# A graph-attention layer on one core: exponentials in mid-step, values 12 steps behind, and the last stage between the last steps

## The chip, the cores and the metric

The kernel runs on one core of a Trainium2 chip. A core has five engines that run their own instruction streams in order: PE (TensorE, matrix products; its weight loads are shown as PEld), DVE (VectorE), ACT (ScalarE), POOL (GpSimd) and SP (SyncE, here used only to issue DMAs). ACT and POOL issue DMAs too, each in its own stream. The metric is the device time of one execution in microseconds (us).

## The reference

One layer of a graph network: 12,500 nodes with 128 channels, 400,000 edges sorted by target node `dst`, 8 heads of 16 channels for the scores and 16 for the values.

```python
h = jnp.maximum(_layernorm(x, axis=-1), 0.0)
msg_src = h @ w_src + b_src
msg_dst = h @ w_dst
message = msg_src[edge_src] + msg_dst[edge_dst]
rad_w = _radial_mlp(edge_scalars, fc_w1, fc_b1, fc_w2, fc_b2, fc_w3, fc_b3)
message = message * edge_attr * rad_w
message = message @ w_sep + b_sep
msg_h = message.reshape(n_edges, H, AH + VH)
alpha = _smooth_leaky_relu(msg_h[:, :, :AH])
value = msg_h[:, :, AH:]
score = jnp.einsum('ehk,ahk->eh', alpha, alpha_dot)
att = _segment_softmax(score, edge_dst, n_nodes)[..., None]   # per target node
out = jax.ops.segment_sum(value * att, edge_dst, num_segments=n_nodes)
x = x + (out.reshape(n_nodes, H * VH) @ w_proj + b_proj)
```

## The kernel before

A first stage normalises the nodes and writes two tables to memory, `t_src` and `t_dst` (the two products of a node). It also counts into `bad` (`fits`, L310) whether the edges are sorted as the fast path needs; every engine then loads `bad` and branches into `windows` (L752).

`windows` walks the edges in steps. A section is 512 edges, a step takes a pair of sections (f = 0 and 1), and there are NP = 391 steps. `step(k)` (L1221) writes out by hand, in one order, what every engine does; several steps are in flight at once:

- two steps ahead POOL issues `gather(k + 2, f)` (L861), eight indirect DMAs a step of 128 rows of `t_src` each, into `gs0` and `gs1` with three buffers each;
- one or two steps ahead come the radial network (`mlp1`, `mlp2`, `mlp3`; silu on ACT), the one-hot rows of the targets and the split target rows (`split_md`);
- in the step itself PE turns the gathered rows into the PSUM tiles `pm0`, `pm1` (`sources`, L929) and adds the target rows (`message`, L937), and DVE multiplies into `mT` (L948), which is the message. `alphas` of the step before (PE, then a silu on ACT, L956) and `scores` every second step (PE, then an Identity on ACT, L987) give the scores;
- a block of MP = 8 steps shares one softmax. Its scores go through memory (`sc_d`) into one tile `S`. In the next block, with r = k mod 8: at the end of r = 2 `softmax_up` (a running maximum on DVE, L1008, over marks that PE spreads into the PSUM tile `m1`), at the end of r = 3 `softmax_down` (the same backwards, L1013) and `softmax_exp` (a subtraction on DVE, an Exp on ACT, L1020, and the maxima written to `max_d`), in r = 4 `softmax_T` in two halves (PE turns the exponentials, L1035, ACT copies them to `Pem`, L1038);
- LAG = 13 steps behind come `values` (PE, L1065, and a product with `Pem` on DVE, L1067) and, 14 behind, `sums` (PE, L1078) into a window of 64 rows for each section, which DVE copies to `ob` (L1082). SP stores the window to `win` and, twice 63 rows, to `agg` (`store`, L1088). The place in `agg` is a run-time value, so each store waits until the one before has landed.

`sums`, `softmax_T`, one half of `mlp1` and the block stages share one PSUM bank, `misc`.

Nodes whose edges lie across section ends are put right by 13 blocks of 128 window ends (`block_load` to `block_rows_out`, two Exps in `block_factors`). Eleven of them run inside the loop, 32 steps apart, and leave their rows in `obs_d`. `scatter(g)` (L1195), an indirect DMA on POOL, writes a block's rows to `agg`.

After the loop, 14 drain steps (k = 391 to 404) finish the values and sums. In each, `combined` brings a block's rows back and POOL scatters them. Then the last block is done, and `final` (L1392) runs over all nodes: it loads `agg` (128 values and 8 denominators a node) and `x` plus the bias (`xb`), divides (`quotients`, L1404), turns (PE and an ACT copy, L1427), multiplies with `w_proj` (PE, L1435), adds (DVE, L1438) and stores `out`.

Of the kernel before, what the change touches and what calls it, by code (L numbers as in the profile page):

```python
# [52 lines left out]
LAG = 13  # L53
# [3 lines left out]
def gnn_kernel(ctx: ExitStack, tc: tile.TileContext, a: dict, out: bass.AP):  # L57
# [9 lines left out]
    NX = -(-NP // MP) * MP * PR  # L67
    assert NT * P == E and RC * RP == E and NT % TPI == 0 and NT % SORT_T == 0
# [88 lines left out]
    with tc.tile_pool(name="node", bufs=2) as np_, tc.tile_pool(name="node1", bufs=1) as n1, \  # L157
# [25 lines left out]
        ends = n1.tile([NH, 17, 2], I32, name="ends")  # L183
        eb = n1.tile([P, NS, 2], I32, name="eb")
# [6 lines left out]
        def load_targets():  # L191
# [118 lines left out]
        def fits():  # L310
# [14 lines left out]
            nc.vector.tensor_copy(bad, sum_)  # L325
# [426 lines left out]
    def windows():  # L752
# [7 lines left out]
        with tc.tile_pool(name="ps", bufs=1, space=PSUM) as pp, \  # L760
# [255 lines left out]
            def softmax_exp(m):  # L1016
                M = Ms[m]
                nc.vector.tensor_sub(M[:, 0, :], S_all[m], M[:, 1, :])
                Ps[m] = sp.tile([P, SEC], F32, name="Pr", bufs=1)
                nc.scalar.activation(Ps[m], M[:, 0, :], AF.Exp)  # L1020
# [66 lines left out]

            def store(c, f):  # L1088
                at = nc.sync.value_load(base[0:1, f, c:c + 1])
                st = nc.sync.dma_start(out=agg[ds(at, W - 1), :], in_=accs[c][f * W:(f + 1) * W - 1, :])  # L1090
                if 2 * c + 1 >= (NC - 1) * (P // 2):
                    tc.declare_no_dep(st.ins, group="combined", reason="its rows follow those of the blocks")
# [45 lines left out]
            def block_maxima(g):  # L1138
                w, node = width(g), nodes.pop(g)
                differ[g] = sp.tile([P, P + 1], BF16, name="differ", bufs=1)  # L1140
# [11 lines left out]
            def block_factors(g):  # L1152
# [5 lines left out]
                nc.scalar.activation(de, de, AF.Exp)  # L1158
                nc.scalar.activation(mx, mx, AF.Exp)
                nc.vector.tensor_mul(mx[:, 1:w:2], mx[:, 1:w:2], differ.pop(g)[:, 1:w:2])  # L1160

            def block_columns(g):
# [7 lines left out]
                mx = mxs.pop(g)  # L1170
                tots[g] = [sp.tile([P, P], F32, name=n, bufs=2) for n in ("rn", "rd")]
# [23 lines left out]
            def scatter(g):  # L1195
# [6 lines left out]
                tc.add_to_no_dep_group("combined", st.ins)  # L1202

            comb = {}

            def combined(g):
                comb[g] = tail_pool.tile([P, ROW], F32, name="comb", bufs=2)
                return comb[g]

            stages = {0: lambda g: (block_load(g), block_rows(g)), 2: block_maxima, 4: block_factors,  # L1210
                      5: block_columns, 6: block_totals, 8: block_out}
            assert LAST_M * MP == (NC - 1) * SB and NP - LAST_M * MP < MP and LATE + (NC - 3) * SB + 8 < NP
# [8 lines left out]
            def step(k):  # L1221
# [63 lines left out]
                if has(c - 1):  # L1285
                    sums(c - 1)
                    if k >= NP:
                        store_win(c - 1)
# [39 lines left out]
                j, o = divmod(k - LATE, SB)  # L1328
                if 0 <= j < NC - 2 and o in stages:
                    stages[o](j)  # L1330

            for k in range(-5, NP):
                step(k)
            held.close()


            tail_pool = held.enter_context(tc.tile_pool(name="fin1", bufs=1, side="right"))
            x_fin = tail_pool.tile([P, NB, C], F32, name="x_fin")
            x_loads = load_xb(x_fin)
            last = NC - 1  # L1340

            def out_rows(g):
                block_rows_out(g, combined(g))
                scatter(g)

# [4 lines left out]
                5: lambda: block_load(last),  # L1350
                6: lambda: block_maxima(last),
                7: lambda: (block_factors(last), block_rows(last - 1)),
                8: lambda: block_columns(last - 1),
                9: lambda: block_totals(last - 1),
                10: lambda: out_rows(last - 1),
            }
            assert SB * (NC - 1) + LAG + 1 == NP + 7
            for k in range(NP, NP + LAG + 1):
# [9 lines left out]
            for _ in x_loads:  # L1368
                pass
            block_rows(last)  # L1370
            block_columns(last)
            block_totals(last)
            out_rows(last)
            work.close()
            with tc.tile_pool(name="fin", bufs=3) as fp:
                final(fp, x_fin, lambda i: pp.tile([P, 4, P], F32, name=("pm0", "pm1", "V")[i % 3]),
                      lambda i: pp.tile([P, 4, C], F32, name=("p3", "pa", "m1")[i % 3]))


    XQ = 12  # L1380
    out_v = out[0:NF * P, :].rearrange("(p t) c -> p t c", t=NF)
    agg_v = agg[0:NF * P, :].rearrange("(p t) c -> p t c", t=NF)

    def load_xb(x_fin):

        for t0, t1 in groups:
            nc.scalar.dma_start(out=x_fin[:, t0:t1, :], in_=xb_v[:, t0:t1, :])
            yield
        nc.scalar.dma_start(out=x_fin[:tail, NF, :], in_=xb[NF * P:N, :])
        yield  # L1390

    def final(fp, x_fin, turned, product):  # L1392
        starts = list(range(0, NB, XQ))
        gs, qs, qTs = {}, {}, {}

        def load_g(i):

            gs[i] = fp.tile([P, XQ, ROW], F32, name="g", bufs=len(starts))
            for n, t0, t1 in blocks(starts[i], min(starts[i] + XQ, NB)):
                o = starts[i]  # L1400
                nc.sync.dma_start(out=gs[i][:n, t0 - o:t1 - o, :],
                                  in_=agg_v[:, t0:t1, :] if n == P else agg[NF * P:N, :].unsqueeze(1))

        def quotients(i):  # L1404
            r = fp.tile([P, XQ, H], F32, name="r")
            qs[i] = fp.tile([P, XQ, C], F32, name="q")
            g = gs.pop(i)
            for n, t0, t1 in blocks(starts[i], min(starts[i] + XQ, NB)):
                s = slice(t0 - starts[i], t1 - starts[i])
                m = t1 - t0  # L1410
                nc.vector.tensor_scalar(r[:n, s, :], g[:n, s, C:ROW], 1e-16, None, op0=ALU.add)  # L1411
                nc.vector.reciprocal(r[:n, s, :], r[:n, s, :])  # L1412
                nc.vector.tensor_mul(  # L1413
                    qs[i][:n, s, :].rearrange("p t (h k) -> p (t h) k", h=H),
                    g[:n, s, 0:C].rearrange("p t (h k) -> p t h k", h=H),
                    r[:n, s, :].unsqueeze(3).to_broadcast([n, m, H, C // H]))

        def turn(i):
            t0, t1 = quads[i]
            q, o = qs[t0 // XQ], t0 // XQ * XQ  # L1420
            pt = turned(i)
            for t in range(t0, t1):
                n = rows(t)
                nc.tensor.transpose(pt[:, t - t0, :n], q[:n, t - o, :], ident[:n, :n])  # L1424
            w = (t1 - t0 - 1) * P + rows(t1 - 1)
            qTs[i] = fp.tile([P, 4, P], F32, name="qT")
            nc.scalar.copy(qTs[i].rearrange("p u n -> p (u n)")[:, :w], pt.rearrange("p u n -> p (u n)")[:, :w])  # L1427

        def finish(i):
            t0, t1 = quads[i]  # L1430
            qT = qTs.pop(i)
            py = product(i)
            for t in range(t0, t1):
                n = rows(t)
                nc.tensor.matmul(py[:n, t - t0, :], qT[:, t - t0, :n], w_proj, start=True, stop=True)  # L1435
            for n, u0, u1 in blocks(t0, t1):
                y = x_fin[:n, u0:u1, :]
                nc.vector.tensor_add(y, py[:n, u0 - t0:u1 - t0, :], y)  # L1438
                nc.sync.dma_start(out=out_v[:, u0:u1, :] if n == P else out[NF * P:N, :].unsqueeze(1), in_=y)

        for i in range(len(starts)):
            load_g(i)
        quotients(0)
        turn(0)
        for i in range(Q):
            if i % 3 == 1 and i // 3 + 1 < len(starts):
# [76 lines left out]
```

## Time and profile before

| | us |
|---|---|
| median of 3 runs | 4211.2 (4210.71 to 4215.71) |
| the profiled execution | 4210.06 |
| its span, first to last instruction | 4208.2 |
| busy in the span: PE, DVE, POOL, ACT | 3917.1, 3103.4, 3009.4, 1901.6 |

In the lines below, "L867" is a line of the kernel, "x8" a number of instructions, and a bracket holds how long the engine sat idle before the instruction and what ended the wait. A matrix product's end is modelled.

### The profile page before, as it was taken

The numbers are of one execution on the slowest core, as the hardware profiler recorded it, in microseconds if no ns is written. First come the engines' busy times: TensorE is split into PE (matmuls) and PEld (weight loads), VectorE is DVE, ScalarE is ACT, GpSimd is POOL, SyncE is SP. The second block draws the span as 40 slices with busy tenths as digits, with TensorE's granted clock in tenths as the row PEclk, the third lists the DMA queues.
The fourth block names the chain that finished last, engine by engine and source line by source line (L and its number), as shares of the span: only waits on it lengthen the run. The fifth ranks groups of instructions, "written<-read, shape, count | busy, mean of one in ns | idle before, by whom it ended". The sixth has DMA issues, their size and how long they took to land. (4 is left out here: it accounts for less than half of the span.)

```text
span 4208.2 us, 87881 instructions
## 1 busy us (share of the span) xinstructions
PE 3917.1 (93%) x29351; PEld 2391.0 (57%) x29351; DVE 3103.4 (74%) x6187; ACT 1901.6 (45%) x4549; POOL 3009.4 (72%) x3195
## 2 busy tenths in 40 slices
PE   6789999999999999999999999999999999999975
PEld 6345555555555555555555555555555555555555
DVE  5567777777777777777777777777777777777754
ACT  5344444444444444444444444444444444444421
POOL 4767777777777777777777777777777777777710
PEclk8999999999999999999999999999999999999988
DMA  7766777777776776777777776776777676776624
GB/s 249 233 173 187 191 187 187 197 192 180 199 192 179 196 195 174 195 195 188 188 192 194 181 193 180 178 188 182 178 191 184 183 184 183 188 180 180 184 84 160
DMA packets 593334, 783.08 MB, mean 186 GB/s; under 512 B 125554, under 2 KB 392303, under 8 KB 592741
## 3 DMA queue, kind: packets, MB, share of 16 engines
q1 hardware_dynamic: 384786, 514.16, 40.9%
q0 software_dynamic: 100416, 205.44, 23.6%
q10 hardware_dynamic: 107666, 57.76, 4.6%
q8 instruction: 234, 3.83, 0.4%
q14 instruction: 232, 1.89, 0.2%
HBM read 637.83 MB, written 139.30 MB: 185 GB/s over the span
## 5 line engine op out<-in xcount | busy, mean ns | idle before, releaser
L867 POOL DMA_INDIRECT gs<-t_src,idx x3125 | 2971.5, 951 | 978.8 <-issue 801.7
L956 ACT ACTIVATE sl<-pa,c_b_a 128x512 f32<-128x512 f32 x782 | 536.9, 687 | 1021.1 <-PE pa L954 1009.5
L961 DVE SCALAR_TENSOR_TENSOR al<-pa,sl 128x512 f32<-128x512 f32 x782 | 539.8, 690 | 596.6 <-ACT sl L956 577.1
L1065 PEld LDWEIGHTS V<-c_w_v,mT 128*128 128x128 f32 x6048 | 746.7, 194 | 292.1 <-DVE ob L1082 119.1
L1065 PE MATMUL V<-c_w_v,mT 128*128 128x128 f32 x6048 | 879.3, 289 | 0.0
L954 PE MATMUL pa<-mT,c_w_a 128*128 128x512 f32 x1564 | 816.1, 604 | 4.0 <-DVE mT L948 3.0
L1067 DVE TENSOR_TENSOR pvx<-V,Pem 128x512 f32<-128x512 f32 x756 | 517.7, 685 | 243.8 <-PE V L1065 232.0
L934 PEld LDWEIGHTS pm<-ident,gs 128*128 128x128 f32 x3125 | 393.0, 142 | 422.1 <-issue 316.9
L1078 PEld LDWEIGHTS misc<-pvx,oh 128*64 128x64 f32 x6250 | 353.0, 137 | 407.8 <-ACT h L890 392.7
L926 DVE SCALAR_TENSOR_TENSOR rad<-p,c_fc_b,w_b 128x512 f32<-128x512 f32 x782 | 550.0, 745 | 40.1 <-PE p L918 3.5
L1078 PE MATMUL misc<-pvx,oh 128*64 128x136 f32 x6250 | 454.2, 287 | 115.4 <-ACT h L890 108.2
L948 DVE SCALAR_TENSOR_TENSOR mT<-pm,c_b_src,rad 128x512 f32<-128x512 f32 x782 | 550.6, 746 | 2.2 <-PE pm L941 2.2
L904 ACT ACTIVATE h<-p,b 128x512 f32<-128x512 f32 x391 | 287.6, 735 | 422.7 <-PE p L901 367.9
L934 PE MATMUL pm<-ident,gs 128*128 128x128 f32 x3125 | 471.0, 273 | 0.0
L918 PE MATMUL p<-h,w3b 64*128 64x512 f32 x1564 | 405.2, 595 | 14.4 <-ACT h L904 14.4
L941 PE MATMUL pm<-ohT,m 64*128 64x512 bf16 x2346 | 321.8, 380 | 0.0
L987 ACT ACTIVATE Sp<-m,b_s 128x512 f32<-128x512 f32 x192 | 131.9, 687 | 393.9 <-PE m L970 389.8
L886 PE MATMUL m<-eT,w1b 64*128 64x256 f32 x782 | 274.3, 431 | 17.9 <-DVE M L1008 16.7
L886 PE MATMUL misc<-eT,w1b 64*128 64x256 f32 x782 | 274.3, 431 | 0.0
L1051 DVE TENSOR_TENSOR oh<-lane,misc 128x504 f32<-128x504 f32 x391 | 261.3, 668 | 0.0
L901 PE MATMUL p<-h,w2b 64*64 64x256 f32 x3128 | 259.7, 402 | 1.0 <-DVE rad L926 1.0
L954 PEld LDWEIGHTS pa<-mT,c_w_a 128*128 128x128 f32 x1564 | 242.2, 196 | 20.0 <-DVE mT L948 7.1
(172 smaller groups left out, 3651.0 us busy)
## 6 DMA issues: line engine op xcount, KB each, us to landing
w_b<-in_edge_weight SPq DMA_DIRECT2D x390, 512.0 KB
d_b<-in_dst SPq DMA_DIRECT2D x390, 256.0 KB
gs<-t_src,idx POOLq DMA_INDIRECT x3125
e_t<-in_edge_attr ACTq DMA_DIRECT2D x390, 128.0 KB
sc_d<-Sp SPq DMA_DIRECT2D x192, 256.0 KB
win<-ob SPq DMA_DIRECT2D x391, 68.0 KB
agg<-ob SPq DMA_DIRECT2D x782, 33.5 KB
md<-t_dst SPq DMA_DIRECT2D x782, 32.0 KB
```

Of the source, the lines that this page charges most:

```text
L867: nc.gpsimd.indirect_dma_start(out=gs[:, t, :], out_offset=None, in_=t_src[:, :], in_offset=bass.IndirectOffsetOnAxis(ap=idx[:, t0 + t:t0 ...
L886: nc.tensor.matmul(p1[q], w1b[s, :], eTs[k][s, :], start=True, stop=True)
L918: nc.tensor.matmul(p3s[k][:, f, 0:SEC], w3b[s, :], h2s[k][s, :], start=True, stop=True)
L926: nc.vector.scalar_tensor_tensor(rad[:, s], p3[:, f, 0:n], b3, w_g[k][:, s], op0=ALU.add, op1=ALU.mult)
L934: nc.tensor.matmul(pms[k, f][:, t * T:(t + 1) * T], gs[:, t, :], ident, start=(t == 0), stop=False, is_transpose=True, skip_group_check=True)
L948: nc.vector.scalar_tensor_tensor(mTs[k][:, s], pms.pop((k, f))[:, 0:n], b_n, rad[:, s], op0=ALU.add, op1=ALU.mult)
L954: nc.tensor.matmul(pa[:, 0:n], w_a, mTs[k][:, f * SEC:f * SEC + n], start=True, stop=True)
L956: nc.scalar.activation(sl[:, 0:n], pa[:, 0:n], AF.Silu, bias=b_a, scale=1.0)
L961: nc.vector.scalar_tensor_tensor(al, pa, 0.25, sl, op0=ALU.mult, op1=ALU.add)
L1065: nc.tensor.matmul(V[:, t, :], mTs[c][:, o:o + T], w_v, start=True, stop=True)
L1067: nc.vector.tensor_mul(pvx[c][:, f, 0:n, 0:C].rearrange("p t (h k) -> p t h k", h=H), V[:, 0:n, :].rearrange("p t (h k) -> p t h k", h=H), ...
L1078: nc.tensor.matmul(acc[f * W:(f + 1) * W, :], ohs[c][:, f * TS + t, :], pvx[c][:, f, t, :], start=(t == 0), stop=(t == n - 1), skip_group_ ...
```

## The change

In the loop, LAG goes from 13 to 12. The softmax of a block moves forward. In r = 2 `softmax_up` stands in mid-step ahead of the second `values`, and `softmax_down` and the subtraction (now `softmax_sub`) at the end. In r = 3 the Exp stands in mid-step, between `mlp1` and `mlp3`, with a block's two Exps (`block_exp`) right behind it where there is one, and both halves of `softmax_T` follow in the same step.

After the loop, the scatters of the 11 early blocks are issued in one go in step NP - 3, behind the last gathers; `bring` loads their rows in four DMAs. The nodes are cut anew into 15 groups (NG) of 875 (125 partitions of 7; the last group has 2 to a partition). In drain step j (k = 391 + j, j = 0 to 12) group j is loaded on ACT's queue, group j - 2 divided, group j - 4 multiplied, added and stored, group j - 3 turned. Two groups are left for the end. `order` tells the scheduler which stores, scatters and loads of `agg` cannot meet; two checks that this holds for the given targets are added to `bad`, with two loads of one word each.

```diff
-LAG = 13
+LAG = 12
...
+                for i, s in enumerate(EARLY_S):
+                    nc.sync.dma_start(out=lim[:, i:i + 1], in_=dst[s * SEC:s * SEC + 1].unsqueeze(1))
...
-            nc.vector.tensor_copy(bad, sum_)
+            low = n1.tile([1, 2], F32, name="low")
+            for i, u in enumerate((EARLY_1, EARLY)):
+                nc.vector.tensor_scalar(low[:, i:i + 1], lim[:, i:i + 1], float(u * GN), None, op0=ALU.is_lt)
+            nc.vector.tensor_add(sum_, low[:, 0:1], sum_)
+            nc.vector.tensor_add(bad, low[:, 1:2], sum_)
...
             def store(c, f):
                 at = nc.sync.value_load(base[0:1, f, c:c + 1])
                 st = nc.sync.dma_start(out=agg[ds(at, W - 1), :], in_=accs[c][f * W:(f + 1) * W - 1, :])
-                if 2 * c + 1 >= (NC - 1) * (P // 2):
-                    tc.declare_no_dep(st.ins, group="combined", reason="its rows follow those of the blocks")
+                order(st.ins, 2 * c)
...
                 if has(k + 2):
                     mlp1(k + 2)
+                j, o = divmod(k - LATE, SB)
+                if has(k - MP) and r == 3:
+                    softmax_exp(m - 1)
+                    if 0 <= j < NC - 2 and o == 5:
+                        block_exp(j)
                 if has(k):
                     mlp3(k)
...
+                if has(k - MP) and r == 2:
+                    softmax_up(m - 1)
                 if has(c):
                     values(c, 1)
-                if has(k - MP) and r == 4:
-                    softmax_T(m - 1, 0)
...
                 if has(k):
                     message(k)
+                if has(k - MP) and r == 3:
+                    softmax_T(m - 1, 0)
                 if has(k + 1):
                     mlp2(k + 1)
-                if has(k - MP) and r == 4:
-                    softmax_T(m - 1, 1)
                 if has(k - MP):
                     if r == 2:
-                        softmax_up(m - 1)
+                        softmax_down(m - 1)
+                        softmax_sub(m - 1)
                     elif r == 3:
-                        softmax_down(m - 1)
-                        softmax_exp(m - 1)
+                        softmax_T(m - 1, 1)
...
             for k in range(-5, NP):
                 step(k)
+                if 0 <= k - (NP - 6) < 4:
+                    bring(k - (NP - 6))
+                if k == NP - 3:
+                    for g in range(NC - 2):
+                        scatter(g)
...
             for k in range(NP, NP + LAG + 1):
                 step(k)
                 j = k - NP
                 if j in jobs:
                     jobs[j]()
-                if 0 <= j - 2 < NC - 2:
-                    nc.sync.dma_start(out=combined(j - 2), in_=obs_d[(j - 2) * P:(j - 1) * P, :])
-                    scatter(j - 2)
+                fn.load_g(j)
+                if 1 <= j <= 4:
+                    fn.load_x(4 * (j - 1), 4 * j - 2)
+                    fn.load_x(4 * j - 2, 4 * j)
+                if j >= 2:
+                    fn.quotients(j - 2)
+                if j >= 4:
+                    fn.finish(j - 4)
                 if j >= 3:
-                    next(x_loads, None)
+                    fn.turn(j - 3)
...
+        def quotients(self, i):
+            g, m = self.g[i], self.tiles(i)
+            r = self.r_tile()[:, 0:m, :]
+            nc.vector.tensor_scalar(r, g[:, :, C:ROW], 1e-16, None, op0=ALU.add)
+            nc.vector.reciprocal(r, r)
+            q = g[:, :, 0:C].rearrange("p t (h k) -> p t h k", h=H)
+            nc.vector.tensor_mul(q, q, r.unsqueeze(3).to_broadcast([GP, m, H, C // H]))
```

The last section's sums no longer go through `win` for the last block: `last_rows` loads what is already there, and `last_rows_2` takes the newest rows from the tile in SBUF.

More of the change, by code (lines that the diff above doesn't have):

```diff
@@ L67, in gnn_kernel @@
     NX = -(-NP // MP) * MP * PR
+    GP, GT = 125, 7
+    GN, NT_F = GP * GT, N // GP
+    NG = -(-NT_F // GT)
+    EARLY_1, EARLY = 11, 13
+    EARLY_S = [(-(-2 * NS // P) - i) * (P // 2) for i in (2, 1)]
     assert NT * P == E and RC * RP == E and NT % TPI == 0 and NT % SORT_T == 0
@@ L1086, in store_win, with order @@
                 nc.sync.dma_start(out=win[c * P:(c + 1) * P, :], in_=accs[c])
+            def order(ins, s, whole=False):
+                i = 1 if s < EARLY_S[0] else 2 if s < EARLY_S[1] else 3
+                for j in (1, 2):
+                    if j < i:
+                        tc.declare_no_dep(ins, group=f"early_{j}", reason="its rows follow those of the earlier sections")
+                    if i <= j:
+                        tc.declare_no_dep(ins, group=f"later_{j}", reason="its rows precede those of the later sections")
+                if whole and i < 3:
+                    tc.add_to_no_dep_group(f"early_{i}", ins)
+                if i > 1:
+                    tc.add_to_no_dep_group(f"later_{i - 1}", ins)
             def store(c, f):
@@ L1328, in step, with bring @@
-                j, o = divmod(k - LATE, SB)
+                        softmax_T(m - 1, 1)
                 if 0 <= j < NC - 2 and o in stages:
                     stages[o](j)
+            def bring(j):
+                g0, g1 = 3 * j, min(3 * j + 3, NC - 2)
+                t = lp.tile([P, 3, ROW], F32, name="e_t", bufs=4)
+                nc.sync.dma_start(out=t[:, 0:g1 - g0, :],
+                                  in_=obs_d[g0 * P:g1 * P, :].rearrange("(g p) c -> p g c", p=P))
+                for g in range(g0, g1):
+                    comb[g] = t[:, g - g0, :]
@@ L1332, in windows @@
+            assert NC - 2 <= 12
             for k in range(-5, NP):
                 step(k)
+                if 0 <= k - (NP - 6) < 4:
[3 more added lines that the diff above has]
+                        scatter(g)
             held.close()
-            tail_pool = held.enter_context(tc.tile_pool(name="fin1", bufs=1, side="right"))
-            x_fin = tail_pool.tile([P, NB, C], F32, name="x_fin")
-            x_loads = load_xb(x_fin)
+            fin = held.enter_context(tc.tile_pool(name="fin1", bufs=1, side="right"))
@@ L1340, in windows, with last_rows @@
+            x_fin = fin.tile([GP, NT_F, C], F32, name="x_fin")
             last = NC - 1
             def out_rows(g):
-                block_rows_out(g, combined(g))
+                comb[g] = sp.tile([P, ROW], F32, name="obk", bufs=1)
+                block_rows_out(g, comb[g])
                 scatter(g)
+            def last_rows():
+                q, s = width(last) // 2, last * (P // 2)
+                rrs[last] = sp.tile([P, ROW], F32, name="rr", bufs=1)
+                for i in range(2):
+                    nc.sync.dma_start(out=rrs[last][i * q:(i + 1) * q - 2, :],
+                                      in_=rows_w[s:s + q - 2, i * (W - 1), :])
@@ L1346, in windows, with last_rows_2 @@
+            def last_rows_2():
+                q = width(last) // 2
+                for i in range(2):
+                    nc.sync.dma_start(out=rrs[last][(i + 1) * q - 2:(i + 1) * q, :],
+                                      in_=accs[NP - 1][i * (W - 1):i * (W - 1) + W + 1:W, :])
             jobs = {
@@ L1371, in windows @@
+                if j >= 2:
+                    fn.quotients(j - 2)
+                if j >= 4:
+                    fn.finish(j - 4)
+                if j >= 3:
+                    fn.turn(j - 3)
+            i = LAG - 1
+            fn.quotients(i)
+            fn.finish(i - 2)
+            fn.turn(i - 1)
             block_columns(last)
+            fn.quotients(i + 1)
             block_totals(last)
+            fn.finish(i - 1)
             out_rows(last)
[L1374 to L1377, printed above, removed]
@@ L1380, in gnn_kernel @@
[L1380 to L1446, printed above, removed]
-                quotients(i // 3 + 1)
-            if i + 1 < Q:
-                turn(i + 1)
-            finish(i)
```

119 lines of the change are left out of this document (92 added, 27 removed).

## The prediction

> **What bounds the kernel now.** I read the page first, then the windows and the one-line view of the gathers, then the order of time of a few steps, then the stretch after the loop.
>
> ```profile
> span 4208.2 us, 87881 instructions
> ```
> ```profile
> L867 POOL DMA_INDIRECT gs<-t_src,idx x3125: 938/944/2392, 73.7 to 4009.5; - x196
> ```
> ```profile
> 300.00:4000.00 3700.00, 2799.11 (x2946) 0.99 0.71 187
> ```
> ```profile
> 300.00:4000.00 3700.00, 518.60 (x736) 0.99 0.71 187
> ```
>
> The second line is the gathers: shortest, median, longest in ns. The two windows are of 300 to 4000 us, first with the gathers alone, then with the products of L948, two to a step: 2946 gathers and 368 steps in 3700 us, so 10.05 us a step and 1.256 us a gather. A gather lasts 0.944 us and its engine rests 0.30 us before the next, in every row of the steady stretch, which makes 1.244; eight are 9.95 us. POOL is thus 1% from filling the loop by itself. PE looks like the limit (93% busy), but both run at one pace.
>
> Where PE loses time is seen in consecutive steps and in the fourth of a block:
>
> ```profile
> 2137.05 1.41 DVE L948 SCALAR_TENSOR_TENSOR mT<-pm,c_b_src,rad 128x512 f32<-128x512 f32 x2
> ...
> 2145.96 1.41 DVE L948 SCALAR_TENSOR_TENSOR mT<-pm,c_b_src,rad 128x512 f32<-128x512 f32 x2
> ...
> 2156.18 1.41 DVE L948 SCALAR_TENSOR_TENSOR mT<-pm,c_b_src,rad 128x512 f32<-128x512 f32 x2
> ...
> 2168.68 1.41 DVE L948 SCALAR_TENSOR_TENSOR mT<-pm,c_b_src,rad 128x512 f32<-128x512 f32 x2
> ```
> ```profile
> 2157.55 1.28 ACT L1020 ACT_TABLE_LOAD   x1
> ...
> 2159.47 0.63 ACT L1020 ACTIVATE Pr<-M 128x512 f32<-128x512 f32 x1 [0.64 <-DVE M L1018]
> ...
> 2160.55 1.28 ACT L956 ACT_TABLE_LOAD   x1
> ...
> 2161.84 0.69 ACT L956 ACTIVATE sl<-pa,c_b_a 128x512 f32<-128x512 f32 x1
> ...
> 2163.16 1.15 PE L1078 MATMUL misc<-pvx,oh 128*64 128x136 f32 x16 [2.17 <-ACT h L890]
> ```
> ```profile
> PE misc L1078 <- ACT h L890: 108.2, 48, 2.6
> ```
>
> The steps k = 202, 203 and 204 take 8.91, 10.22 and 12.50 us. In 204 (r = 4) ACT loads the Exp's table, waits for DVE, computes, and loads the silu's table back before it reaches the silus PE needs: PE stands 2.17 us in front of the sums, and this happens 48 times. That step is 3.6 us longer than its plain neighbour.
>
> **The change part by part: the loop.** The Exp now comes after `mlp1`'s silus in a step with scores (r = 3 is odd). ACT has two holes there:
>
> ```profile
> 2131.18 0.48 ACT L890 ACTIVATE h<-m,b 128x256 f32<-128x256 f32 x1
> 2133.73 0.69 ACT L987 ACTIVATE Sp<-m,b_s 128x512 f32<-128x512 f32 x1 [2.07 <-PE m L970]
> 2135.71 0.69 ACT L956 ACTIVATE sl<-pa,c_b_a 128x512 f32<-128x512 f32 x1 [1.29 <-PE pa L954]
> ```
>
> Load and Exp are 1.28 + 0.63 = 1.91 us in a hole of 2.07; the load back is 1.28 in a hole of 1.29. So ACT hides them behind PE's sums, scores and second values, with nothing to spare; a block's two Exps (0.6 us, every fourth time) push the silu by half a microsecond. Uncovered, they cost up to 3.2 us a block, what they cost now.
>
> [...]
>
> `softmax_up` in mid-step must find `S` landed, since DVE stops at it and behind it stand the second value product, an `al` sum and `mT`, for which PE waits.
>
> ```profile
> 219.15 0.58 SPq L993 DMA_DIRECT2D S<-sc_d  x1
> ...
> 222.70 1.22 DVE L1008 TENSOR_TENSOR_SCAN M<-m,S 128x512 f32<-128x512 f32 x1 [16.37 <-DMA S<-sc_d]
> ...
> 229.87 0.94 POOL L867 DMA_INDIRECT gs<-t_src,idx  x1 [9.15 <-PE m L877]
> ```
> ```profile
> 2136.59 0.56 SPq L993 DMA_DIRECT2D S<-sc_d  x1
> ...
> 2143.65 0.17 DVE L1054 TENSOR_TENSOR oh<-misc,far 128x8 f32<-128x8 f32 x1
> ```
>
> The one time DVE waited for it, `S` came 3.55 us after its issue. In a steady block it is issued at 2136.6, so it lands near 2140.1, and the scan's new slot opens behind L1054 at 2143.8: 3.7 us to spare. Two scans and a subtraction put 3.1 us on DVE in r = 2, of which about half spills into r = 3, where DVE has 2 us free. PE's share (two spreads, four turns, about 1 us) stays. I set the new stalls at 0.5 us a block, so a block of eight steps should fall by about 3 us, from 80.4 to 77.4.
>
> But POOL needs 8 x 9.95 = 79.6 to 80.3 (with its own uneven gathers; rests longer than 0.30 us come to some 3 us after 300 us). PE will catch up with the gathers within ten blocks and then wait for them. **The loop's end is set by the last gather.**
>
> ```profile
> 4009.50 0.94 POOL L867 DMA_INDIRECT gs<-t_src,idx  x1 [0.30 <-PE V L1065]
> ```
> ```profile
> 4031.20 0.60 PE L934 MATMUL pm<-ident,gs 128*128 128x128 f32 x4
> ...
> 4037.25 1.00 DVE L948 SCALAR_TENSOR_TENSOR mT<-pm,c_b_src,rad 128x512 f32<-128x512 f32 x2
> ```
>
> Now the last gather ends at 4010.4 and the last `mT` at 4038.2, 27.8 us later. When PE waits for gathers, step 390's first turns start as they land, and from there (4031.20) to the last `mT` is 7.05 us: 7 instead of 27.8, a gain of 21. At the start it costs something: in step 10 the first `S` comes late, POOL then stops 9.15 us on its buffers, and with the wait ahead of L877 in the step instead of behind it POOL stops four gathers sooner, 5 us (between 0 and 9). The two one-word loads of `lim` stand in SP's queue ahead of the tables: 1 us. POOL's own waits give back 3 (0 to 20, if all above 1.25 us were waits). Last `mT`: 4038.2 - 21 + 6 - 3 = **4020**.
>
> **The drain.**
>
> ```profile
> 4038.00:4125.00 87.00, 56.49 (x448) 46.10 (x448) 37.73 (x92) 10.83 (x40) 9.76 (x10) 0.80 0.35 109
> 4125.00:4142.00 17.00, 1.16 (x5) 0.62 (x5) 0.67 (x4) 0.56 (x2) 2.84 (x3) 0.61 0.31 97
> 4142.00:4202.00 60.00, 39.86 (x294) 37.91 (x294) 38.50 (x56) 14.38 (x25) 0.00 (x0) 0.88 0.51 196
> ```
>
> Columns: length, PE, PEld, DVE, ACT, POOL busy, PE's granted clock, DMA share, GB/s. Fourteen steps take 87 us, 6.2 each, with 4.0 us of PE and 2.7 of DVE. The last stage takes 60 us for 98 tiles of nodes; seven of the new 100 tiles are 2.8 us of PE, 2.7 of DVE, 1.0 of ACT. A drain step that carries both has 6.8 us of PE at these clocks (5.7 at the full clock, which 0.80 and 0.88 scale to) and 5.4 of DVE, in two streams that feed each other a step apart. I take 6.2 a step for the eight full ones, 25 for the first four (the old mean), 3 into the last: 78.
>
> Two things add. The scatters, 11 x 1.27 = 14 us behind the last gather, hold the first group's load on ACT's queue until about 4029; the copies of `Pem` behind it are a step early, so this is covered. The loads of `x` are 6.4 MB in four steps:
>
> ```profile
> 4060.00:4073.00 13.00, 12.47 (x109) 10.98 (x107) 5.54 (x12) 2.09 (x10) 1.02 (x1) 0.87 0.84 284
> ```
> ```profile
> 4113.28 1.83 SPq L1090 DMA_DIRECT2D agg<-ob  x2
> ```
> ```profile
> SPq L1090 <- DMA agg<-comb,ids: 21.3, 4, 11.9
> ```
>
> Quiet, a pair of stores takes 1.83 us in SP's queue. In the 13 us at 284 GB/s (the old loads of `x`) one store waited 11.9 us for a scatter. No scatter stands between now, but a store's landing then takes 6 rather than 1.5 us, and DVE stops when the three `ob` are used up. I add 5 (0 to 15). From the last `mT` to the last `ob`: **83** (87 before).
>
> **The end.**
>
> ```profile
> 4124.61 0.30 DVE L1082 TENSOR_TENSOR ob<-misc,bare 128x136 f32<-128x136 f32 x1 [1.10 <-PE misc L1078]
> ...
> 4142.28 0.21 DVE L1411 TENSOR_SCALAR r<-g 128x96 f32<-128x96 f32 x1 [8.15 <-issue]
> ...
> 4143.31 1.76 DVE L1413 TENSOR_TENSOR q<-g,r 128x1536 f32<-128x1536 f32 x1
> ...
> 4149.09 0.69 DVE L1438 TENSOR_TENSOR x_fin<-p,x_fin 128x512 f32<-128x512 f32 x1 [4.02 <-PE p L1435]
> ...
> 4201.20 0.47 DVE L1438 TENSOR_TENSOR x_fin<-p,x_fin 128x128 f32<-128x128 f32 x2
> ```
>
> Before: 17.4 us from the last `ob` to the first division, 59.4 of last stage, 6.5 from the last sum (4201.7) to the span's end; 83.3 in all. Now two groups, of 7 and 2 tiles, are left. The way to their load keeps block, scatter and load; it loses the trip through `win` (3) and gains the groups queued among its pieces (3): 17. Division of 7 tiles 1.6, then 4.2 to the first sum (before: 4.0 for eight tiles, plus 0.7), 0.6 for the second half, 2.5 for the small group, 6.5 as before: **32**.
>
> Sum: 4020 + 83 + 32 = 4135 us of span. The profiled execution has 1.9 us around its span and lies 1.1 below the median of the runs shown; I forecast **4137 us**, 74 less than the median. Bounds of the unknown costs: start -6 and +4, POOL's waits -17 and +3, drain steps at 5.7 or 6.8, x loads -5 and +10: 4105 to 4160.
>
> **The rivals.**
>
> Second: the loop keeps its pace, since the Exp is not covered or PE stands somewhere else for 3 us a block (ACT's holes fit to 0.01 us, which speaks for it; the slack of `S` against it). Then the last `mT` is at 4039 with the start's cost partly hidden, and the end at 4039 + 83 + 32 + 2 = 4156.
>
> Third: POOL's rest of 0.30 us is a wait that shrinks when PE is faster. Then the loop takes 48 x 3 = 144 us less: about 4137 - 144 + 18 = 4011. Against it: the rest is the same in fast and slow steps, and nothing in 2946 gathers is quicker.
>
> Fourth, the other side: the pair of stores. If with loads of groups, loads of `x` and stores of `out` the landing stays at 6.5 us through all 13 steps, a step takes 2 x 6.5 + 0.9 = 13.9 us, and the end is 4020 + 181 + 32 + 2 = 4235. It turns slower than before at 12.2 us a step. For it: 284 GB/s and the 11.9 us wait. Against it: a step moves about 1 MB, and at 6.3 us that is 160 GB/s, where (4142 to 4202) 196 were moved at half share.
>
> Fifth, the change doesn't do what it says: the groups' loads are held behind the stores of their own step after all, ACT's stream stops with them, and a step becomes store pair, landing and turn, about 9 us: 4020 + 117 + 32 + 2 = 4171.
>
> **How the numbers follow.** Forecast 0.58, second 0.17, third 0.07, fourth 0.10, fifth 0.08. The range from 4098 to 4174 holds the forecast's own 4105 to 4160, the second and the fifth, and leaves out the third and the fourth. A difference of 0.2% (8.4 us) is about what a measurement of this kernel can tell from none. Faster: 0.58 + 0.17 + 0.07 + 0.08 less 0.02 of their tails = 0.88; same 0.02; slower 0.10, the fourth.
>
> **What would show it.** Right: the step r = 4 near 9.1 us and no wait of L1078 for the silu; PE waiting for `gs` in the later loop, with the last gather 6 to 8 us before the last `mT`; gathers still 1.25 us apart; drain steps of 6 to 6.5 us with PE near its full clock; some 32 us from the last `ob` to the end. Wrong: gathers closer than 1.24 us, a wait of L1008 for `S` in steady blocks, drain steps of 9 us and more with SP waiting for `agg<-ob`, or ACT waiting there for `g`.

## The result, and the profile after the change

The kernel after the change takes 4224.94 us (median of 10 runs, 4221.83 to 4242.39), the kernel before beside it 4211.74 us (median of 10): a ratio of 1.0036, with a 95% interval of 1.0026 to 1.0045. It is 0.4% slower, a small difference that is clear of the runs' scatter; the forecast was 4137 us. The profiled execution took 4227.18 us. In two of the sets of runs below (the kernel before beside them: 5309.6 and 5315.8 us) the loop of every kernel ran slower by a quarter, the one before too, for a reason that stays open; of these sets only the stages behind the loop are compared with others.

First the loop. These are, after the change, the page's first line, the one-line view of the gathers, the last gather, the last `mT` and the list of waits (us in total, times, longest).

```profile
span 4225.3 us, 87959 instructions
```
```profile
L879 POOL DMA_INDIRECT gs<-t_src,idx x3125: 940/944/2375, 75.1 to 4012.7; - x196
```
```profile
4012.74 0.94 POOL L879 DMA_INDIRECT gs<-t_src,idx  x1 [0.30 <-PE pm L946]
```
```profile
4021.69 1.00 DVE L960 SCALAR_TENSOR_TENSOR mT<-pm,c_b_src,rad 128x512 f32<-128x512 f32 x2
```
```profile
PE pm L946 <- DMA gs<-t_src,idx: 70.0, 76, 3.2
...
DVE M L1020 <- DMA S<-sc_d: 19.9, 1, 19.9
...
PE misc L1092 <- ACT h L902: 15.7, 27, 1.1
```

The last gather ends at 4013.7 and the last `mT` at 4022.7, 9.0 us later (27.8 before). PE now waits for `gs`, 76 times and up to 3.2 us, and the sums' wait for the silu has fallen from 108.2 us to 15.7. The last `mT` stood at 4038.2 before and was forecast at 4020, so the loop gave what was forecast of it, but for 3 us.

The loss lies behind it. From the last `mT` to the last `ob` (4159.2) it takes 136.5 us, where 87 were before and 83 were forecast; from there to the end 66.2 us, where 83.3 were before and 32 were forecast. The windows of that stretch, with the columns of the prediction's (length, busy time of PE, PEld, DVE, ACT and POOL, PE's granted clock, DMA share, GB/s):

```profile
4022.00:4060.00 38.00, 22.18 (x166) 16.81 (x166) 19.17 (x41) 6.46 (x14) 4.56 (x5) 0.85 0.32 111
4060.00:4125.00 65.00, 27.47 (x192) 25.53 (x193) 19.44 (x46) 6.12 (x23) 0.00 (x0) 0.66 0.34 127
4125.00:4175.00 50.00, 32.50 (x277) 30.02 (x276) 28.77 (x58) 7.95 (x23) 1.63 (x1) 0.81 0.33 112
4175.00:4226.00 51.00, 16.21 (x88) 13.90 (x88) 10.16 (x22) 3.87 (x9) 0.90 (x1) 0.63 0.25 81
```

No engine is full, and yet the steps take 10.5 us on average (4.6 to 23.3 from one `ob` to the next). The DMA share is the odd column: 0.32, 0.34, 0.33, with 111 to 127 GB/s, as flat as a ceiling, though the last stage before moved 196 GB/s at 0.51. If it is one, transfers queue under it, and the engines' streams with them. The order of time has SP's pairs of stores and ACT's loads of `x`, the waits say for what:

```profile
4031.01 6.73 ACTq L1476 DMA_DIRECT2D x_fin<-xb  x4
...
4069.28 11.20 ACTq L1476 DMA_DIRECT2D x_fin<-xb  x4
4080.52 0.58 ACT L1507 COPY h<-V 128x500 f32<-128x500 f32 x1 [17.35 <-DMA win<-ob]
```
```profile
4094.46 10.72 SPq L1116 DMA_DIRECT2D agg<-ob  x2
4105.28 0.28 SPq L1516 DMA_DIRECT2D out<-x_fin  x1
4108.43 0.36 SPq L1100 DMA_DIRECT2D win<-ob  x1
4110.14 10.03 SPq L1116 DMA_DIRECT2D agg<-ob  x2
```
```profile
ACT h L1507 <- DMA win<-ob: 17.3, 1, 17.3
ACT h L1507 <- DMA out<-x_fin: 14.6, 1, 14.6
```

A pair of stores takes 5.4 to 10.7 us in most steps, where the quiet pair took 1.83. ACT's copies stand up to 17.3 us behind DMA issues in ACT's own stream. And the chain that ended last shows what the last two groups waited for: the scatter's landing and then their own load's. The rows to be scattered (`obk`) were ready only 28.7 us after the last `ob`.

```profile
4187.59 0.26 ACT L1216 COPY obk<-misc 28x136 f32<-28x136 f32 x1 [4.08 <-PE misc L1215]
```
```profile
4188.16 9.43 DMA agg<-obk,ids
...
4197.65 7.72 DMA mT<-agg
```

### The profile page after: what moved, and what is told of

It is laid out like the page before. It is cut to its first block, busy times and chain, and to the rows that moved or that the text cites. A ratio compares the mean times of both kernels' runs of the same rounds, so it can differ in the third digit from the quotient of the medians.

```text
span 4225.3 us, 87959 instructions
## 1 busy us (share of the span) xinstructions
PE 3932.9 (93%) x29357; PEld 2383.0 (56%) x29357; DVE 3094.7 (73%) x6208; ACT 1895.0 (45%) x4553; POOL 3009.4 (71%) x3195
## 5 line engine op out<-in xcount | busy, mean ns | idle before, releaser
L1079 PEld LDWEIGHTS V<-c_w_v,mT 128*128 128x128 f32 x6064 | 738.0, 192 | 298.6 <-DVE ob L1096 153.4
L1079 PE MATMUL V<-c_w_v,mT 128*128 128x128 f32 x6064 | 868.1, 286 | 0.0
L966 PE MATMUL pa<-mT,c_w_a 128*128 128x512 f32 x1564 | 804.3, 596 | 3.9 <-DVE mT L960 2.8
L938 DVE SCALAR_TENSOR_TENSOR rad<-p,c_fc_b,w_b 128x512 f32<-128x512 f32 x782 | 550.3, 745 | 118.0 <-PE p L930 86.7
L946 PE MATMUL pm<-ident,gs 128*128 128x128 f32 x3125 | 492.5, 275 | 71.7 <-DMA gs<-t_src,idx 70.0
L1092 PE MATMUL misc<-pvx,oh 128*64 128x136 f32 x6250 | 455.8, 288 | 25.4 <-ACT h L902 15.7
L902 ACT ACTIVATE h<-misc,b 128x256 f32<-128x256 f32 x391 | 193.1, 494 | 144.2 <-PE misc L898 141.3
```

The costliest lines, as they stand in the source:

```text
L938: nc.vector.scalar_tensor_tensor(rad[:, s], p3[:, f, 0:n], b3, w_g[k][:, s], op0=ALU.add, op1=ALU.mult)
L946: nc.tensor.matmul(pms[k, f][:, t * T:(t + 1) * T], gs[:, t, :], ident, start=(t == 0), stop=False, is_transpose=True, skip_group_check=True)
L966: nc.tensor.matmul(pa[:, 0:n], w_a, mTs[k][:, f * SEC:f * SEC + n], start=True, stop=True)
L1079: nc.tensor.matmul(V[:, t, :], mTs[c][:, o:o + T], w_v, start=True, stop=True)
L1092: nc.tensor.matmul(acc[f * W:(f + 1) * W, :], ohs[c][:, f * TS + t, :], pvx[c][:, f, t, :], start=(t == 0), stop=(t == n - 1), skip_group_ ...
```

## The experiments

The question: why does everything land late? Theory A, five engines: a transfer of 125 partitions is spread over 5 of the 16 DMA engines (5/16 = 0.31). Rival B, order: ACT and SP stop since each DMA waits for an earlier one to land, and the number and the order of the transfers decide. Rival C, bytes: the 19 MB of the groups' loads and stores are what the memory takes.

All runs are in one table. `g124`, `g126`, `spread125` and `nox125` are one execution each. "Drain" is from the last `mT` to the last `ob`, "end" from there to the last instruction, each from the profiled execution, and "total" is the median.

| kernel | groups | drain | end | both | total | before, beside it |
|---|---|---|---|---|---|---|
| before | | 86.7 | 83.3 | 170.0 | 4211.7 | |
| after | 125 by 7 | 136.5 | 66.2 | 202.7 | 4224.9 | 4211.7 |
| `g128` | 128 by 7 | 88.7 | 29.7 | 118.4 | 5159.4 | 5309.6 |
| `g128b` | 128 by 7 | 92.8 | 31.8 | 124.6 | 4147.5 | 4208.5 |
| `g126` | 126 by 7 | 95.5 | 38.6 | 134.1 | 5173.9 | 5309.6 |
| `g124` | 124 by 7 | 164.7 | 73.9 | 238.7 | 5271.6 | 5309.6 |
| `loop` | as before | 79.3 | 84.5 | 163.7 | 5199.7 | 5309.6 |
| `loopb` | as before | 76.9 | 84.4 | 161.4 | 4184.5 | 4208.5 |
| `spread125` | 125 by 7 | 126.1 | 78.5 | 204.6 | 4232.1 | 4208.5 |
| `spread128` | 128 by 7 | 79.8 | 37.1 | 116.9 | 4142.7 | 4208.5 |
| `nox125` | 125 by 7 | 104.8 | 64.6 | 169.4 | 4189.4 | 4209.0 |
| `pair128` | 128 by 7 | 92.0 | 31.0 | 123.0 | 4143.4 | 4209.0 |
| `xpool128` | 128 by 7 | 86.3 | 32.0 | 118.3 | 4143.2 | 4209.0 |
| `best128` | 128 by 7 | 84.4 | 41.1 | 125.5 | 5176.9 | 5315.8 |

**The number of partitions.** `g128` and `g128b`, and with the first line changed `g124` and `g126`:

```diff
-    GP, GT = 125, 7
-    GN, NT_F = GP * GT, N // GP
-    NG = -(-NT_F // GT)
+    GP, GT = 128, 7
+    GN = GP * GT
+    cut = [(g * GN, GP, GT, g * GT) for g in range(N // GN)]
+    left = N % GN
+    if left // GP:
+        cut.append((N - left, GP, left // GP, len(cut) * GT))
+    if left % GP:
+        cut.append((N - left % GP, left % GP, 1, cut[-1][3] + cut[-1][2]))
+    NG, NT_F = len(cut), cut[-1][3] + 1
...
-                nc.scalar.dma_start(out=self.x[:, i * GT:i * GT + self.tiles(i), :], in_=self.view(xb, i))
+                nc.scalar.dma_start(out=self.x[:cut[i][1], cut[i][3]:cut[i][3] + self.tiles(i), :], in_=self.view(xb, i))
```

> Only the shape of the groups changes: 13 of 896 nodes (128 partitions by 7 nodes), one of 128 by 6 and one of 84 by 1, in place of 14 of 875 (125 by 7) and one of 125 by 2. The bytes, the queues and the order stay. Theory A (five engines): after the change the DMA share stands at 0.32 to 0.34 and the rate at 111 to 127 GB/s from 4022 to 4175 us, which is what 5 of 16 engines give (5/16 = 0.31), where the kernel before reached 0.53 and 200 GB/s; a transfer of 125 partitions uses as many engines as divide its 125 rows. With 128 rows the share goes over 0.40 wherever several loads are out, ACT no longer stops at the loads of x, SP's pairs of stores fall under 4 us; last mT to last ob 85 to 105 us (136.5 now), last ob to the end 35 to 50 us (66 now), total 4140 to 4180 us. Rival B (order): ACT and SP stop because each new DMA waits for one issued some places before it, whatever engines carry it; the number and order of transfers is the same, so the total is 4210 to 4235 us. Rival C (bytes): 19 MB are what the memory takes in that time; the same bytes, 4215 to 4235 us. [...]

> Groups of 124 partitions by 7 (868 nodes, 14 of them, then 124 by 2 and 100 by 1): one partition fewer than after the change. Theory A: 124 is 4 times 31, so four engines carry the large transfers in place of five; the 19 MB of loads and stores take 5/4 of the 147 us that they take at 130 GB/s, so 25 to 45 us longer, total 4245 to 4275 us, DMA share 0.24 to 0.30 between 4022 and 4175 us. Rivals B and C: the same transfers and bytes but for one small group more, total 4220 to 4240 us.

> Groups of 126 partitions by 7 (882 nodes, 14 of them, then 126 by 1 and 26 by 1): one partition more than after the change. Theory A: 126 is 14 times 9, so 14 engines; within 15 us of the kernel with 128 partitions, total 4140 to 4190 us. Rivals B and C: as after the change, 4215 to 4240 us.

> The kernel with groups of 128 by 7 once more. In the first run of it every kernel's loop ran slower, the kernel before at 5309 us; where the kernel before takes 4211 us, this one takes 4022 to 4024 us to the last mT, 89 from there to the last ob and 30 to the end: 4140 to 4150 us. Should the loop be slow again, the last two terms are as in the first run within 5 us.

The windows of the middle of the drain, of the kernels with 124, 126 and 128 (`g128b`):

```profile
5070.00:5135.00 65.00, 21.08 (x146) 19.73 (x147) 13.55 (x33) 4.71 (x18) 0.00 (x0) 0.63 0.28 109
```
```profile
5077.00:5133.00 56.00, 45.27 (x402) 42.29 (x403) 37.88 (x84) 11.47 (x38) 1.63 (x1) 0.87 0.62 196
```
```profile
4060.00:4115.00 55.00, 45.23 (x403) 42.27 (x404) 38.00 (x85) 11.49 (x38) 1.64 (x1) 0.88 0.58 195
```

One partition fewer than 125 makes both stages together 36 us longer (238.7), one more makes them 69 us shorter (134.1), and the share goes from 0.34 to 0.28 and to 0.62. Work, bytes and order are all but the same, so B and C can't do that. 124 = 4 x 31, 125 = 5 x 25, 126 = 14 x 9, 128 = 16 x 8: theory A holds.

The traces' records of single packets say the same directly, when one counts how many packets of 2 KB and more (the groups' loads and stores) are under way at one moment of these windows. With 124 partitions it is four in 79% of the time. With 125 (4060 to 4125 us) it is five in 67%, and in 85% of the moments in which SP's queue and ACT's queue both have some out; so loads and stores share five places. With 126 and 128 the most frequent number, but for none at all, is 14 and 16. A packet is no slower with 125 (0.140 us in the median) than with 128 (0.148): only fewer run at once. Five packets of 3584 bytes in 0.140 us are 128 GB/s; the windows after the change show 127 at most.

In `g128b` SP's pairs, the last rows to be scattered and the last load read:

```profile
4080.99 3.77 SPq L1122 DMA_DIRECT2D agg<-ob  x2
...
4095.32 1.79 SPq L1122 DMA_DIRECT2D agg<-ob  x2
...
4107.61 1.85 SPq L1122 DMA_DIRECT2D agg<-ob  x2
```
```profile
4124.39 0.26 ACT L1222 COPY obk<-misc 28x136 f32<-28x136 f32 x1 [3.11 <-PE misc L1221]
```
```profile
4128.13 3.55 DMA mT<-agg
```

The pairs take 1.8 to 5.0 us, the rows are ready 9.4 us after the last `ob`, and the load lands after 3.55 us where it took 7.72. Three details of A's expectation for `g128` missed: the end is shorter than 35 to 50 us, not all pairs fall under 4 us, and ACT still stands at a bunch of loads of `x` (14.2 us in `g128`, 15.2 in `g128b`), which is B's part. Against the kernel before, `g128b` has a ratio of 0.9849 (0.9832 to 0.9865), `g128` 0.9719 (0.9683 to 0.9755); the second is not to be compared with the first, since in its set `loop` alone has 0.9786 (0.9740 to 0.9832).

**The loop alone**, with the drain and the last stage of the kernel before (the diff shows the LAG; the softmax, block and `step` parts are those of the change):

```diff
-LAG = 13
+LAG = 12
...
-                5: lambda: block_load(last),
-                6: lambda: block_maxima(last),
-                7: lambda: (block_factors(last), block_rows(last - 1)),
+                3: lambda: block_exp(last - 1),
+                4: lambda: block_load(last),
+                5: lambda: block_maxima(last),
+                6: lambda: (block_factors(last), block_exp(last), block_rows(last - 1)),
```

> The loop's part of the change alone: LAG of 12, the exponentials in mid-step, softmax_T in step 3; the steps after the last gather and the last stage are those of the kernel before. By the prediction's terms the last mT comes at 4020 to 4024 us (4038.2 before), and there are 13 steps to drain in place of 14, so the total is 4190 to 4198 us. Rival D: what the loop gains is waited for again later, by the stores and loads of the drain, total 4204 to 4213 us.

> The loop's part of the change alone once more. Where the kernel before takes 4211 us: last mT 4020 to 4024 us, then 79 and 84 us as in the first run, total 4185 to 4190 us. Rival D, as before: 4204 to 4213 us.

`loopb` takes 4184.47 us, a ratio of 0.9942 (0.9925 to 0.9958): 24 us less, half a microsecond under its expectation. Its last `mT` ends at 4022.1, 16 us sooner, and the drain of 13 steps is 10 us shorter; rival D falls. The first expectation, 4190 to 4198, lies 6 us and more too high: less the 1.8 us around the span, it left 168 to 172 us for what follows the last `mT`, which took 161.4. So the new last stage, not the loop, cost the time: with 125 by 7 the kernel is some 40 us slower than `loopb`, with 128 by 7 it is 37 us faster.

**The order of the loads of x.** One load to a step in place of bunches of four, with 125 and with 128:

```diff
-                if 1 <= j <= 4:
-                    fn.load_x(4 * (j - 1), 4 * j - 2)
-                    fn.load_x(4 * j - 2, 4 * j)
+                if j >= 1:
+                    fn.load_x(j - 1, j if j < LAG else NG)
```

> The kernel after the change with its groups of 125 by 7, but the loads of x one to a step (group j - 1 in step j, the last three in step 12) in place of four in each of four steps. Theory A (five engines): the loads and stores of the groups are 19 MB, at 130 GB/s 147 us whatever their order, so last mT to the end stays at 190 to 205 us (202.7 after the change). Rival B (order): ACT stopped 6.7, 7.0, 11.2 and 9.4 us at its four bunches of loads, 34 us in all; with one load to a step it doesn't, and last mT to the end is 160 to 172 us.

> Groups of 128 by 7 and the loads of x one to a step. In the run with 128 by 7 alone one drain step still took 18.6 us (from the ob of 5076.2 to that of 5094.7), in which ACT stood 14.2 us at loads of x; the last steps took 5.3 to 6.2 us. Theory A with the bunch as the rest of it: that step falls to 6 to 8 us, last mT to last ob 74 to 82 us (88.7 with 128 by 7 alone), the end as there (29.7 us). Rival: the wait is the engines' and only moves, 86 to 90 us.

With 125 ACT's stops at the bunches are gone but for the last four loads, and both stages together still take 204.6 us (202.7): what was not waited for there was waited for elsewhere, by DVE 20.1 us for `node` and by ACT 16.55 us at the last bunch:

```profile
DVE differ L1166 <- DMA node<-ends_d: 20.1, 1, 20.1
```
```profile
4159.05 16.55 ACTq L1475 DMA_DIRECT2D x_fin<-xb  x4
```

B falls as the first cause. With 128 the drain fell to 79.8 us as expected, but the end grew to 37.1, where the last four loads of `x` now stood (with none of them there, in `pair128` below, it is 31.0); 4142.73 against 4147.53 us is inside what the runs scatter.

**Without the loads of x**, with 125 (the product alone is stored):

```diff
-                nc.scalar.dma_start(out=self.x[:, i * GT:i * GT + self.tiles(i), :], in_=self.view(xb, i))
+            pass
...
-                nc.vector.tensor_add(y, py[:GP, 0:b - a, :], y)
+                nc.vector.tensor_copy(y, py[:GP, 0:b - a, :])
```

> The kernel after the change with its groups of 125 by 7, without the loads of x: the output is the product alone, x and the bias are not added. Theory A (five engines): 6.4 of the 19 MB are gone, at 130 GB/s 49 us, so last mT to the end is 150 to 160 us (202.7 after the change). Rival B (order): what ACT stood at its four bunches of loads is gone, 34 us, and last mT to the end is 165 to 172 us. Rival E (stores): the pairs of stores into agg set the step by themselves, 190 us or more.

Both stages together: 169.4 us, 33 less, not the 49 that A forecast from the bytes; it lies in B's range. The window shows why the bytes were the wrong measure:

```profile
4060.00:4125.00 65.00, 37.88 (x317) 35.13 (x316) 37.19 (x82) 7.90 (x26) 1.64 (x1) 0.82 0.31 99
```

The rate fell to 99 GB/s, so the stretch was not filled with transfers any more (no large packet is under way in 16% of it, 3% after the change); each one is still slow (the pairs of stores take up to 8.14 us), and the steps wait for one after the other. A sets how long a transfer lasts; how many of them a step waits for is a matter of the order, as B has it.

**Other orders with 128.** Two loads of `x` to a step; on POOL's queue; and one to a step with the last block's maxima a step later.

```diff
+                if 1 <= j <= 8:
+                    fn.load_x(2 * (j - 1), 2 * j)
```
```diff
+                if 1 <= j <= 5:
+                    fn.load_x(3 * (j - 1), 3 * j)
...
-                nc.scalar.dma_start(out=self.x[:cut[i][1], cut[i][3]:cut[i][3] + self.tiles(i), :], in_=self.view(xb, i))
+                nc.gpsimd.dma_start(out=self.x[:cut[i][1], cut[i][3]:cut[i][3] + self.tiles(i), :], in_=self.view(xb, i))
```
```diff
+                if 1 <= j <= 9:
+                    fn.load_x(j - 1, j)
+                elif j >= 10:
+                    fn.load_x(2 * j - 11, 2 * j - 9)
...
-                5: lambda: block_maxima(last),
-                6: lambda: (block_factors(last), block_exp(last), block_rows(last - 1)),
-                7: lambda: block_columns(last - 1),
+                6: lambda: (block_rows(last - 1), block_maxima(last)),
+                7: lambda: (block_columns(last - 1), block_factors(last), block_exp(last)),
```

> Groups of 128 by 7, the loads of x two to a step in steps 1 to 8. With one to a step the end took 37.1 us (29.7 and 31.8 with the bunches) since the last four loads stood in step 12, where the DMA share was 0.78 to 0.82. Theory A, as a limit on engines that are now all in use: last mT to last ob 79 to 84 us, the end 30 to 32 us, total 4134 to 4141 us. Rival: a gain in the end is lost in the drain, total 4141 to 4147 us.

> Groups of 128 by 7, the loads of x on POOL's queue, three to a step in steps 1 to 5; POOL has nothing else to do there until a scatter in step 9. With the loads on ACT's queue ACT stood 15.2 us (bunches) and 9.8 us (one to a step) at them. Theory: ACT no longer stops, and last mT to last ob is 70 to 78 us, the end 30 to 32 us, total 4126 to 4134 us. Rival: the loads take the engines from the stores and the groups' loads all the same, and the drain is 79 to 86 us as with the other orders.

> Groups of 128 by 7, the loads of x one to a step in steps 1 to 9 and two in 10 to 12, and the maxima of the last block a step later, behind which DVE stood 5.8 to 8.4 us for the load of node. Theory: that step falls from 11 to 14 us to 6 to 8, last mT to last ob is 72 to 77 us, the end 30 to 34 us, total 4128 to 4136 us. Rival: the step is held by the stores and loads around it as well, and the total stays at 4140 to 4147 us, as in the other orders with 128 by 7.

None beats the others: 4143.39 and 4143.19 us (0.9845 both, 0.9829 to 0.9861 and to 0.9862), and 0.9734 (0.9702 to 0.9766) where `g128` had 0.9719. The drains were to fall to 79 to 84, 70 to 78 and 72 to 77 us, and took 92.0, 86.3 and 84.4. Each time one wait goes and another comes. On POOL's queue the loads of `x` came early and met the last block's `S` and a pair of stores, which took 13.1 us: ACT waited 12.1 us for the `M` that needs `S`. With the maxima later, ACT waited 11.5 us for `rr`:

```profile
ACT Pr L1036 <- DVE M L1040: 12.1, 1, 12.1
```
```profile
ACT rx L1198 <- DMA rr<-win: 11.5, 1, 11.5
```

So the rivals hold in all three (in `best128` by its stages): the kernel with 128 by 7 stands at 4142 to 4148 us in the four orders that ran beside a kernel before of 4209 us, about 1.5% faster than before and 1.9% faster than the change.

## Why the prediction was wrong, step by step

**The loop ends with the last gather: right.** Forecast 4020 for the last `mT`, measured 4022.7. The gathers kept their 0.944 us and their pace (2947 in the 3700 us from 300 on, 2946 before), so the third rival falls. The start's cost is right too: POOL stops 13.81 us for its buffers where it stopped 9.15, 4.7 more (5 forecast), and DVE waits for `S` just that once. The term that was too small is the way from the last gather to the last `mT`, 9.0 us instead of 7.

**The Exp is hidden in ACT's holes: half right, and of no consequence.** The first load and the Exp went where they were put. The load back did not:

```profile
2138.78 1.28 ACT L1030 ACT_TABLE_LOAD   x1
2140.08 0.63 ACT L1030 ACTIVATE Pr<-M 128x512 f32<-128x512 f32 x1
2140.65 0.69 ACT L999 ACTIVATE Sp<-m,b_s 128x512 f32<-128x512 f32 x1
2142.61 1.28 ACT L968 ACT_TABLE_LOAD   x1 [1.27 <-PE pa L966]
...
2143.91 0.69 ACT L968 ACTIVATE sl<-pa,c_b_a 128x512 f32<-128x512 f32 x1
```

It stands behind the wait for `pa` (1.27 us idle, then the load), so the hole of 1.29 us passed unused and the silu came 1.3 us late. That step (r = 3) took 11.7 us (from the `mT` of 2133.52 to that of 2145.24), and the next (r = 4), which was to come near 9.1, took 12.3 (to 2157.57); PE waited 1.6 us for gathers in it. With the gathers as the pace this cost nothing: eight steps still take their 80 us.

**The drain: wrong, and this is the step that failed.** Of the 90 us of span that the forecast lacked, the loop has 3, the drain 53 and the end 34. The prediction held against the fourth rival that "a step moves about 1 MB, and at 6.3 us that is 160 GB/s, where (4142 to 4202) 196 were moved at half share", and took 5 us for all contention (the landing of 6 us behind it is in no row; a pair then took 5.4 to 10.7 in most steps). The 196 GB/s had been moved by transfers of 128 partitions. The new ones have 125, and their ceiling here was 111 to 127 GB/s; at that rate 1 MB alone is 8 to 9 us. With 126 or 128 partitions the very same steps drain in 89 to 96 us, and the window has 195 GB/s. The width of 125 stood in the change as it was described; the prediction took it for a matter of PE's and DVE's tiles and never asked what it does to a transfer.

**The end: the sum was right for other transfers.** 32 forecast, 66.2 measured, 29.7 and 31.8 with 128 by 7. In `g128b` its parts fit as well: 16.4 us from the last `ob` to the first division of the last two groups (17 forecast) and 15.4 from there (15.4 by its terms). After the change the first part took 46.2 us. The scatter's landing (9.43) and the load's (7.72) are in it, but most is the 28.7 us before `obk` is ready, where SP's stream holds two pairs of stores (4.80 and 3.92) and the small loads of `rr`, for which ACT waited 12.4 us. The sum's last line has a slip that decides nothing: its 1.9 and 1.1 us would make 4138 of 4135.

**The fourth rival** came nearest in time (4235) and named the right place: SP's pairs, whose wait the drain is full of. But its cause was the load on memory, and its price 13.9 us a step; measured are 10.5, and the pairs are slow because of the width of other transfers, since with 128 by 7 and the same order they take 1.8 to 5.0. **The fifth** saw ACT stop, which it did; `spread125` shows that the stops at `x` alone are not the cause. The second was not met: the loop did not keep its pace.

The sum with the shape mended, 4022.5 + 92.8 + 31.8 = 4147 us of span in `g128b`, lies 12 us over the forecast's 4135. The steps at full pace take 5.3 to 6.0 us there, but three take 9.8, 11.2 and 21.0 us. In the second DVE stands 4.4 us before the scan over `S`, in the last ACT stands 15.2 us at a bunch of loads of `x`; with 125 that last step took 23.3. So the order's part is left also where the width is right, and the mean of 6.2 left it out.

## What to carry to other kernels

Before a transfer's time is taken from another one's rate, compare the partitions: 124 and 125, whose largest divisors up to 16 are 4 and 5, held the DMA share at 0.28 and 0.34 here, where 126 and 128 reached 0.62 and 0.58. The last load took 7.72 us with 125 and 3.55 with 128, a pair of stores 5.4 to 10.7 us in most steps against 1.8 to 5.0. The sign was a DMA share that stayed flat a little over a simple fraction (0.34 for 5/16, 0.28 for 4/16) while engines idled. A stage that is laid between the steps of a loop brings its landings with it; sum the transfers that each step must wait for, not just the engines' busy time.

## What the runs showed of the hardware that was not expected

In the four numbers of partitions that ran, the DMA share in the middle of the drain goes with the largest divisor up to 16: 0.28 for 124 (4/16 = 0.25), 0.34 for 125 (5/16 = 0.31), 0.62 for 126 and 0.58 for 128, where the transfers no longer fill the time. Small packets add to it: with 125 those under 2 KB are 0.05 of the 0.34. The large packets under way at once, counted above, agree: 4, 5, 14 and 16. Why the divisor decides is not shown, and no full group had another number of partitions. That loads and stores share the same five is an inference from the five packets at once with both queues out (85% of those moments); the records do not name the engines.

An issue of a load of `x` takes 0.26 us in the median; one took 4.18 us, and what held it is not shown:

```profile
L1476 ACTq DMA_DIRECT2D x_fin<-xb x15: 257/262/4176, 4031.0 to 4089.3; - x15
```

Most of ACT's stops lie between the issues. In the trace after the change the DMAs that SP and ACT issue signal eight semaphores (486 or 487 DMAs each), and before each of the 102 issues from 4022 us on its engine waits on the semaphore that it will signal, so for the DMA that used it before. The load of `x` issued at 4034.69 us starts 0.03 us after a row of `S`, issued on SP's queue at 4029.15, has landed; ACT had stood 3.2 us since its last issue. So here a slow transfer on one queue stopped the other queue's engine. It is read from the trace and was not tried by itself.
